# A cross-attention block whose written-out order is exchanged for another one

## The chip, the cores and the metric

The kernel runs on one core of one Trainium2 chip. The metric is the device time of one execution in microseconds (us). A core has five engines with instruction queues of their own: PE multiplies matrices, DVE (VectorE), ACT (ScalarE) and POOL (GpSimd) work element by element, and SP issues the transfers between the chip's memory and the on-chip memory (SBUF). PE's results land in the banks of a second on-chip memory (PSUM).

## The reference

One transformer layer with cross attention, all in float32. The inputs are `x` and `ctx`, each 8 x 256 x 512 (8 batches of 256 tokens, 512 features), and a mask over the context's tokens; there are 16 heads of 32, and the inner width is 2048. What is computed, cut to its core:

```python
x = layer_norm(hidden_states, ln1_w, ln1_b)
q = x @ q_w + q_b;  k = ctx @ k_w + k_b;  v = ctx @ v_w + v_b      # per head
attn = softmax(where(mask, q @ k.T / sqrt(32), lowest))
hidden = (attn @ v) @ cproj_w + cproj_b + hidden_states
y = layer_norm(hidden, ln2_w, ln2_b)
y = gelu(y @ fc_w + fc_b) @ proj_w + proj_b
return hidden + y
```

## The kernel before, in words

The tokens are worked through in two groups, `g` = 0 and 1, of 1024 tokens (four batches) each. In each group the kernel transposes the context (`turned`, L710, for group 0), forms keys, values and queries, runs attention in 16 units of four heads and one batch (`scores`, L1009, and `attend`, L1057), applies the output projection, and then the two large products: `fc` (L1184, 512 to 2048, with gelu) and `proj` (L1248, 2048 to 512). The two groups overlap: attention of group 1 runs beside `fc` of group 0, and so on.

Every large product is made from seven smaller ones instead of eight (Strassen's scheme in Winograd's form). `quad` (L848) writes one such scheme: products `P1` to `P7` go to three PSUM banks X, Y and W, and element-wise steps `t1`, `t2`, `t3`, `c11`, `c12`, `c21`, `c22` take them out and add them up. The sums of operands that the scheme needs are made beforehand by `sums` (L827) through `plus` (L621): for example `kws1` to `kws4` from the key weights, `fw...` from the weights of fc, `pw...` from those of proj, `y...` and `z...` from the activations. For fc and proj the scheme is used on two levels, so that `fc104_P3` is the product P3 within the outer product 4 of the fc of group 1 (half 0), and `pd11_P5` the product P5 within the outer product 1 of the proj of group 1. The sums of the weights are stored to the chip's memory once (`fcd`, `prd`) and loaded again when they are used (`fl...`, `pl...`).

The helpers that the profile names: `mm` (L636) issues the matmuls of a product (L639), `plus` an addition (L630, on POOL L628 in two halves where it is 1024 wide), `take` and `copy` (L606, L619) a copy out of PSUM, `load` (L590, L593) and `store` (L596, L599) one transfer each on SP. `less` inside `scores` (L1042 on DVE, L1047 on POOL) takes the row maxima off the scores ahead of the exponential.

No scheduler orders the work when the kernel is built. The order is written out by hand in a string `PROGRAM`: 2953 words, one for each operation. The method `run` (L94) reads it. Each engine issues its operations in the order in which their words stand, and a letter behind a colon names the engine where two can do it: `V` is DVE, `A` ACT, `G` POOL. A second string, `PLACES` (L355), gives 1286 buffers their place: a number is a slot of SBUF (or a bank of PSUM), and `C0` or `W1` a bank lent from the other set of banks. A wide SBUF slot of 1024 is an even number n and covers the half slots n and n + 1. Two buffers with one place follow each other: the later one is filled when the last reader of the earlier one is done. PSUM has banks W (3) and C (5).

```python
        for word in PROGRAM.split():
            name, _, e = word.partition(":")
            o = ops.pop(name)
            o.eng = letters[e] if e else o.alts[0][0]
...
    with tc.manual_schedule():
        for o in order:
            o.fn(o.eng)
```

All transfers go through the one queue of SP, in order: a load whose slot is not free yet holds up all that stands behind it. Eight transfers can be outstanding.

At the start, `cq...` loads the context, `turn_c0_...` transposes it, `vw..` and `kw..` load weights of values and keys, and `v0_0_P1` is the first large product. At the end, `ending` (L1293) finishes the last quarter: `tr1_..` transposes results on DVE into `tq`, `out1_..` adds the residual, `so1_..` store `tq` in pieces of 128 KB; the last product `pd14_P4` comes out in the layout of the output (in the profile its tile is `pd_V`), `turn_o..` are PE transposes of the rest, `ot..` and `oz` add, and `st1`, `st00` and `st01` store.

Of the kernel before, what the change touches and what calls it, by code (L numbers as in the profile page):

```python
# [124 lines left out]
cq0_00_1 cq0_00_0 vw00 cq0_01_1 cq0_01_0 rows8 rows7 cq0_10_0 turn_c0_00 rows0 turn_c0_10 c0_00:A cq0_10_1 c0_10:V  # L125
cq0_11_0 small v0_0_P1 cq0_11_1 kw01 turn_c0_11 fw0_01_0 v0_1_P1 c0_11:A vw11 rows5 turn_c0_01 rows2 turn_c0_30
vw10 c0_01:A turn_c0_20 mk c0_30:A c0t1:G c0_20:V v0_0_t1:A vw01 turn_c0_21 v0_1_t1:V turn_c0_31 fw0_11_1 k0_0_P2
c0_21:V rows3 c0_31:V c0t2:V kw10 k0_1_P2 rows4 kw11 c0t3:V kw00 rows6 v0_0_P2 vws1:V fw0_10_0 c0t4:V fw0_00_0
v0_1_P2 vws2:V fw0_00_1 kws1:V xt0_3 rows1 k0_1_P1 fw0_10_1 kws2:V mk~1 xt0_0 kws3:V fw0_11_0 v0_0_c11 fw0i1_1:G
v0_1_P6 fw1_00_1 vws4:V xt0_2 fw0i1_2:V fw0s3:V fw1_00_0 k0_0_P1 v0_1_t2:A xt0_6 fw0i7_1:V fw1_10_0 v0_1_c11  # L130
fw0i7_2:G fw1_11_0 cols v0_1_P5 cols~1 qw10 k0_0_t1:V qw11 fw0i7_4:V fw0s1:V xt0_1 v0_0_P6 v0_1_t3:A fw1_11_1
fw0s2:V fw1_10_1 xt0_5 k0_0_P6 fw0i6_3:V xt0_4 k0_1_t1:V fw0i6_1:G cb fw0i5_1:G v0_1_P3 k0_0_t2:V kws4:G fw0i1_4:V
k0_1_P6 stats_x0_30 fw0i1_3:G fw1i1_1:V stats_x0_00 fw0i6_2:G k0_0_P5 fw1i1_3:V k0_1_t2:A xt0_7 v0_0_t2:V fw1i1_2:G
fw0_01_1 stats_x0_10 fw1i1_4:G fcd0_1_True aggr_x0_30 k0_1_P5 fw1i4_1:V qw01 aggr_x0_00 stats_x0_01 fw1i4_2:G
fw1_01_0 fw0i6_4:V fcd0_6_False stats_x0_11 k0_1_P7 k0_1_t3:A fw1_01_1 aggr_x0_01 fw0i7_3:V k0_0_t3:A eps_x0_0
fcd0_7_False stats_x0_31 pow_x0_0 qw00 aggr_x0_31 k0_1_P3 fw1i4_4:G k0_1_c22 fcd0_7_True fw0i5_2:G aggr_x0_11
fcd0_5_False nb_x0_0 k0_0_c11 fw0i5_4:G norm_x0_01:A v0_0_P5 aggr_x0_10 k0_1_c11 fw0i2_1:G norm_x0_00:A fw1i4_3:V
k0_1_c12:A fw0i2_2:V k0_0_P7 eps_x0_1 eps_x0_3 fw0i5_3:V stats_x0_20 pow_x0_3 stats_x0_21 pow_x0_1 k0_0_P3 nb_x0_3
nb_x0_1 fw0i2_3:V norm_x0_31:A aggr_x0_20 aggr_x0_21 eps_x0_2 fw0i2_4:V norm_x0_10:A pow_x0_2 k0_0_c22 fcd0_2_True
k0_1_P4 v0_0_t3:V fw1i2_1:G fcd1_4_True k0_0_c12:A fcd0_6_True norm_x0_11:A nb_x0_2 fw0s4:V kd0_0_11 k0_0_P4  # L140
fcd1_1_True vws3:V norm_x0_20:A fcd0_3_False fw1i2_2:V fcd0_5_True norm_x0_21:A qws1:V turn_x0_10 norm_x0_30:A
fw1i2_4:G k0_0_c21 turn_x0_00 x0_10:A turn_x0_20 turn_x0_30 x0_20:A v0_0_P3 x0_30:V qws3:G xt1_2 cb1_02 x0_00:V
v0_1_c12:A fw0i3_1:V turn_x0_31 fw1i2_3:V turn_x0_11 fw0i3_2:V x0_31:A turn_x0_21 fw1s1:V turn_x0_01 q0_0_P1
x0_01:A qws2:G v0_0_c12:V fcd1_5_False x0_21:A k0_1_c21 fcd1_2_True fw1i5_3:G cb1_20 x0_11:A q0_0_P2 cb1_03
q0_0_t1:A x0t1:V q0_1_P1 fw0i3_3:V q0_0_c11 x0t2:V s000 fw0i3_4:V x0t3:V q0_0_P6 ev000_11 ev000_31 fw1s3:V xt1_3
ev000_10 ev000_01 cb1_12 q0_0_P7 x0t4:V kd0_0_21 q0_0_t2:A fcd1_7_False q0_1_t1:A fw1s2:V ev000_21 ev000_00 q0_0_P5
mx000_0 fw1s4:G fcd1_6_False cb1_10 q0_1_P6 q0_0_t3:A ev000_30 q0_0_c22 ev000_20 stats_x1_10 fcd1_3_False q0_1_P2
fw1i3_3:V fw1i5_1:V q0_1_t2:V fw1i5_2:G mx000_1 q0_0_P4 fw1i6_1:G qws4:G q0_1_c11 q0_1_P5 q0_0_c21 fw1i5_4:V mt000
fw0i4_3:G fcd1_5_True mc000_3 mc000_2 s020 cb1_13 mc000_1 fw1i6_3:G fold000 cb1_00 fw1i7_1:V q0_0_P3 md000 ev020_30
fw0i4_1:V ev020_21 fw1i7_2:V cb1_23 ev020_00 fw0i4_2:G cb1_21 ev020_10 fw1i7_4:G ev020_20 cb1_01 q0_1_P7 ev020_01  # L150
cb1_11 fw1i3_1:G ev020_31 q0_0_c12:A mx020_1 fw1i6_2:G ev020_11 s002 fw1i3_2:G mm000 mx020_0 fw0i4_4:G v0_1_P7
fw1i7_3:G mt020 stats_x1_11 mc020_2 mc020_3 fw1i6_4:G q0_1_t3:V ev002_30 ev002_11 fw1i3_4:G aggr_x1_10 aggr_x1_11
v0_0_P7 mc020_1 q0_1_c22 ev002_01 ev002_00 fold020 ev002_10 eps_x1_1 md020 ev002_31 pow_x1_1 ev002_20 q0_1_P3
fcd1_7_True v0_0_c22 ev002_21 cb1_31 nb_x1_1 mx002_0 less000_1:G mm020 s022 mx002_1 cb1_33 cb1_22 v0_0_P4 ev022_20
cT1_10 cb1_32 ev022_30 cT1_00 ev022_11 cb1_30 less000_0:G ev022_31 mt002 v0_1_c22 ev022_21 q0_1_P4 ev022_00 mx022_1
mc002_2 ev022_01 ev022_10 less020_0:G mx022_0 v0_1_P4 mt022 q0_1_c21 mc022_2 mc022_3 s010 mc022_1 v0_0_c21 mc002_3
exp000_0 less020_1:G cT1_01 k1_0_P1 fold022 mc002_1 ev010_20 q0_1_c12:V md022 exp000_1 v0_1_c21 fcd1_6_True cT1_20
fcd1_3_True k1_1_P1 ev010_10 ev010_31 fold002 ev010_11 cT1_11 md002 cT1_30 av000 vd0_0_11 k1_0_t1:A cT1_21 mm022
c1t1:G ev010_21 kd0_0_12 ev010_01 cT1_31 ev010_30 kd0_1_12 exp020_0 k1_0_P2 r000 mm002 ev010_00 exp020_1 att000
c1t2:V s030 norm_x1_11:A c1t3:V av020 xd1_3 ev030_10 norm_x1_10:A fcd0_4_True less022_1:G mx010_1 ev030_11 xd1_2  # L160
# [195 lines left out]
cq0_00=42 cq0_10=78 cq0_01=10 cq0_11=0 ps_cols=4 ps_c0_00=2 c0_00=36 ps_c0_10=3 ps_c0_20=3 c0_10=48 ps_c0_30=2  # L356
ps_c0_01=0 c0_01=16 ps_c0_11=3 ps_c0_21=4 c0_11=72 ps_c0_31=0 xt0_0=71 xt0_1=46 xt0_2=47 xt0_3=60 xt0_4=15 xt0_5=14
# [1141 lines left out]
```

## Time and profile before

| | before |
|---|---|
| device time, median of 3 runs | 665.8 us (665.53 to 665.96) |
| span of the profiled execution | 662.0 us |
| PE busy | 654.6 us, 99% |
| DVE busy | 585.7 us, 88% |
| POOL busy | 374.8 us, 57% |
| ACT busy | 342.4 us, 52% |
| moved by DMA | 144.84 MB, 219 GB/s on average |

The span reaches from the first to the last record of one execution. The profile shows no separate device time for this one execution; the device times of the three runs are 3.5 to 4.0 us above its span.

Busy times are totals over the whole span. The profile's windows give the same for a stretch of time: its start and end, its length, the busy time of PE, PE's weight loads (PEld), DVE, ACT and POOL with the number of their instructions, the clock granted to PE, the share of the DMA engines' time and the GB/s. A row of a list of waits names an engine, a tile and line that waited, what it waited for, and the time in total, the number and the longest. A row of a timeline gives start, length, engine, line, operation and tiles, with the idle time before it and what ended that.

### The profile page before, as it was taken

Reading aid. Unit: us, or ns where it says so; the run is one execution under the profiler, and the core shown is the slowest. Engines: PE = TensorE matmul, PEld = TensorE weight load, DVE = VectorE, ACT = ScalarE, POOL = GpSimd, SP = SyncE. Lnnn points to the kernel's source line nnn. Section 1 sums busy time; section 2 is a strip of 40 time slices with the busy share of each in tenths; the row PEclk is TensorE's granted clock in tenths of the full one; section 3 lists DMA queues with packets and bytes.
Section 4 is the critical chain, followed back from the end, with each engine's and each line's share of the span. In section 5 each row is a group of like instructions: output and inputs, shape, how many; then the busy total and the mean of one; then the engine's idle time right before and its main releaser. Section 6 shows DMA issues by size and latency. Waiting matters only on the chain.

```text
span 662.0 us, 11469 instructions
## 1 busy us (share of the span) xinstructions
PE 654.6 (99%) x3925; PEld 490.0 (74%) x3925; DVE 585.7 (88%) x980; ACT 342.4 (52%) x702; POOL 374.8 (57%) x340
## 2 busy tenths in 40 slices
PE   8999999999999999999999999999999999999997
PEld 7746554477544776777688888888888888888887
DVE  2998799999999999999999998997789787998775
ACT  2046479799999899866995572030020013930000
POOL 1262773646888997699958774423535217720260
PEclk9999999999999999999999999999999999999999
DMA  8999888786574467886878698889978779359366
GB/s 250 311 356 307 211 197 291 267 255 125 144 241 161 144 202 234 263 268 197 266 249 273 198 235 225 289 269 230 195 193 241 190 201 242 93 142 240 106 141 111
DMA packets 206586, 144.84 MB, mean 219 GB/s; under 512 B 117008, under 2 KB 166976, under 8 KB 206528
## 3 DMA queue, kind: packets, MB, share of 16 engines
q1 hardware_dynamic: 206528, 144.11, 76.8%
q8 instruction: 31, 0.51, 0.3%
q14 instruction: 27, 0.22, 0.1%
HBM read 104.10 MB, written 39.98 MB: 218 GB/s over the span
## 4 chain that ended last, share of the span: by engine, by line
PE 92%; DVE 5%; ACT 1%; DMA 1%; issue 0%; SPq 0%; POOL 0%; DVEq 0%; ACTq 0%
PE pd_X L639 15%; PE fc_X L639 14%; PE fc_W L639 8%; PE av L639 7%; PE pd_W L639 7%; PE s L639 4%; PE o_X L639 4%; PE q_X L639 4%; PE k_X L639 4%; PE v_X L639 4%; PE pd_Y L639 4%; PE fc_Y L639 4%; PE q_W L639 2%; PE k_W L639 2%; PE v_W L639 2%; PE o_W L639 2%
## 5 line engine op out<-in xcount | busy, mean ns | idle before, releaser
L1047 POOL TENSOR_TENSOR pr<-pr,mm 128x512 f32<-128x512 f32 x84 | 110.4, 1346 | 22.8 <-DMA mm<-md 9.2
L619 ACT ACTIVATE pr<-s,cols 128x256 f32<-128x256 f32 x256 | 104.5, 482 | 21.8 <-PE s L639 15.8
L1022 DVE TRANSPOSE_TENSOR_REDUCE mx<-pr 128x32 f32<-128x1024 f32 x64 | 77.6, 1223 | 3.3 <-ACT pr L619 3.3
L1227 ACT ACTIVATE h<-h,cols 128x256 f32<-128x256 f32 x128 | 54.1, 498 | 36.7 <-DVE h L630 36.6
L1050 ACT ACTIVATE pr<-pr 128x1024 f32<-128x1024 f32 x64 | 66.9, 1069 | 3.4 <-POOL pr L1047 2.8
L630 DVE TENSOR_TENSOR h<-fc_X,h 128x512 f32<-128x512 f32 x80 | 52.8, 679 | 6.2 <-PE fc_X L639 5.5
L630 DVE TENSOR_TENSOR h<-fc_W,h 128x512 f32<-128x512 f32 x48 | 32.0, 679 | 5.8 <-PE fc_W L639 5.3
L639 PE MATMUL av<-pr,ones 128*32 128x256 f32 x512 | 34.2, 384 | 0.7 <-ACT pr L1050 0.6
L1029 ACT COPY mx<-mx 32x64 f32<-32x64 f32 x96 | 23.1, 243 | 19.8 <-DVE mx L1026 15.8
L1042 DVE TENSOR_TENSOR pr<-pr,mm 128x1024 f32<-128x1024 f32 x22 | 30.8, 1407 | 0.0
L628 POOL TENSOR_TENSOR z1i<-h,z1i 128x512 f32<-128x512 f32 x4 | 5.7, 1440 | 40.4 <-PE pd_X L639 40.4
L639 PEld LDWEIGHTS av<-pr,ones 128*32 128x32 f32 x512 | 14.1, 109 | 18.5 <-issue 6.7
L630 POOL TENSOR_TENSOR h<-h,fl 128x512 f32<-128x512 f32 x9 | 11.5, 1295 | 24.6 <-DVE fl L630 15.0
L639 PE MATMUL fc_W<-y1i,fl 128*128 128x256 f32 x100 | 24.6, 380 | 0.0
L639 PE MATMUL fc_X<-y1i,fl 128*128 128x256 f32 x88 | 21.6, 381 | 0.0
L639 PEld LDWEIGHTS fc_W<-y1i,fl 128*128 128x128 f32 x100 | 18.9, 190 | 2.9 <-DVE h L630 0.3
L639 PE MATMUL pd_W<-z0i,pl 128*128 128x256 f32 x88 | 20.6, 379 | 0.0
L1030 DVE TENSOR_REDUCE mx<-mx 32x32 f32<-32x256 f32 x32 | 18.4, 574 | 1.4 <-ACT mx L1029 1.3
L639 PE MATMUL pd_X<-z0i,pl 128*128 128x256 f32 x80 | 18.9, 379 | 0.0
L606 ACT COPY fl<-fc_X 128x512 f32<-128x512 f32 x6 | 3.5, 580 | 29.5 <-PE fc_X L639 29.2
L639 PEld LDWEIGHTS fc_X<-y1i,fl 128*128 128x128 f32 x88 | 16.6, 190 | 2.6 <-ACT h L606 0.2
L639 PEld LDWEIGHTS pd_W<-z0i,pl 128*128 128x128 f32 x88 | 16.7, 190 | 2.3
(595 smaller groups left out, 1815.6 us busy)
## 6 DMA issues: line engine op xcount, KB each, us to landing
mm<-md SPq DMA_DIRECT2D x32, 512.0 KB, 5.1
pl<-prd SPq DMA_DIRECT2D x47, 256.0 KB, 4.2
fl<-fcd SPq DMA_DIRECT2D x41, 256.0 KB, 4.0
fl<-prd SPq DMA_DIRECT2D x24, 256.0 KB, 3.8
fw<-in_L_xattn_fc_w_dram SPq DMA_DIRECT2D x16, 256.0 KB, 4.9
pw<-in_L_xattn_proj_w_dram SPq DMA_DIRECT2D x32, 128.0 KB, 3.6
hid<-in_x_dram SPq DMA_DIRECT2D x8, 512.0 KB, 4.8
hd<-hid SPq DMA_DIRECT2D x8, 512.0 KB, 3.4
```

The costliest lines, as they stand in the source:

```text
L606: (nc.scalar.copy if e == "ACT" else nc.vector.tensor_copy)(to(), of_())
L619: lambda e: nc.scalar.activation(to(), of_(), AF.Identity, bias=bias(), scale=1.0))
L628: nc.gpsimd.tensor_tensor(to()[:, ts(k, 512)], in0()[:, ts(k, 512)], in1()[:, ts(k, 512)], op)
L630: E[e].tensor_tensor(to(), in0(), in1(), op)
L639: nc.tensor.matmul(o(), l(), r(), start=first, stop=True, skip_group_check=True)
L1022: T.op(f"mx{u}_{h}", [("DVE", 1.126)], [(pr[h], None)], [(mx, [h])], lambda e, h=h: nc.vector.tensor_reduce(tile_of(mx)[:, 0:64].rearrange ...
L1029: lambda e, a=a: nc.scalar.copy(tile_of(mx)[0:32, 64 + 64 * a : 128 + 64 * a], tile_of(mx)[32 * a : 32 * a + 32, 64:128]))
L1030: T.op(f"fold{u}", [("DVE", 0.38)], [(mx, [2, 3, 4, 5])], [(mx, [6])], lambda e: nc.vector.tensor_reduce(tile_of(mx)[0:32, 320:352], tile_ ...
L1042: nc.vector.tensor_tensor(p_, p_, m_[:, :, None, :].to_broadcast([P, 2, 2, S]), ALU.subtract)
L1047: E[e].tensor_tensor(p_, p_, at(M, j)[:, None, :].to_broadcast([P, 2, S]), ALU.subtract)
L1050: lambda e, h=h: nc.scalar.activation(tile_of(pr[h]), tile_of(pr[h]), AF.Exp), table="exp")
L1227: lambda e, f=f, b=b, c=c: nc.scalar.activation(at(h[f][b], c), at(h[f][b], c), AF.Gelu_apprx_tanh, bias=col(c_fcb + f * 4 + c), scale=1.0 ...
```

## The change

All functions stay as they are. `PROGRAM` and `PLACES` are replaced as wholes. The 2953 words are the same but for the engine letters. Of the operations, 223 change engine: 98 go from DVE to POOL, 67 from POOL to DVE, 34 from ACT to DVE and 24 from DVE to ACT. By number of operations DVE goes from 913 to 892, ACT from 692 to 682 and POOL from 250 to 281; PE keeps its 500 and SP its 598. Nearly every buffer has another slot or bank. PE's operations keep their order roughly: 101 of 500 stand at the same position in PE's own sequence, 357 within three places of it, and none is more than 34 places away.

The first words of the order, before and after:

```diff
-cq0_00_1 cq0_00_0 vw00 cq0_01_1 cq0_01_0 rows8 rows7 cq0_10_0 turn_c0_00 rows0 turn_c0_10 c0_00:A cq0_10_1 c0_10:V
-cq0_11_0 small v0_0_P1 cq0_11_1 kw01 turn_c0_11 fw0_01_0 v0_1_P1 c0_11:A vw11 rows5 turn_c0_01 rows2 turn_c0_30
...
+cq0_00_1 small cq0_00_0 turn_c0_00 turn_c0_10 cq0_01_1 cq0_01_0 vw00 c0_10:V vw10 vws3:V turn_c0_01 c0_00:A cq0_11_0
+turn_c0_11 c0_11:V vw11 cq0_11_1 cq0_10_1 c0_01:V c0t1:V rows5 v0_0_P1 v0_1_P1 kw00 cq0_10_0 turn_c0_21 turn_c0_31
...
```

The last words (in before, seven large products stand behind `pd12_P4`, in the new order two; the words from it on are shown):

```diff
...
-out1_01:V pd12_P4 pl14_5 pd12_c12 tr1_01 out1_00:V pd17_12~1:V pd14_P6 so1_01 tr1_13 so1_03 so1_22 so1_20 pd13_P4
-pd14_t2 so1_23 pd12_c21 z1i4_3:V so1_31 so1_02 pd14_P5 pd13_c21 tr1_12 out1_11:V tr1_11 pd14_P2 tr1_10 out1_10:V pd14_t3
-so1_13 pd14_P7 so1_12 pd14_c11 so1_10 so1_11 so1_00 pd14_P3 pd14_c22 pd14_c21 turn_o00 pd14_c12 turn_o10 turn_o11 ot00
-turn_o01 ot11 pd14_P4 st00 ot10 ot01 st1 oz st01
...
+out1_11:V pd12_P4 so1_31 pd14_t3 tr1_11 pd14_P3 pd14_c21 pd14_c22 rl1 turn_o11 pd12_c21 tr1_10 turn_o10 so1_33
+turn_o00 out1_10:V pd14_c12 turn_o01 ot00 so1_21 out1_00:G so1_02 so1_01 so1_00 ot10 so1_12 so1_03 ot11 so1_13 so1_11
+ot01 st1 st00 so1_10 z1i4_4:G pd14_P4 oz st01
```

Among the products of group 1 this sequence stands on PE in the new order: `pd11_P6`, `fc104_P3`, `fc104_P4`, `fc114_P4`, `fc114_P3`, `pd11_P5`. Some of the places that change, cut to single entries:

```diff
-pl06_3=86
-h0_20=72
-pl11_6=57
-pl11_5=35
-pl12_2=59
-pl15_6=44
+pl06_3=39
+h0_20=38
+pl11_6=32
+pl11_5=32
+pl12_2=38
+pl15_6=38
```

More of the change, by code (lines that the diff above doesn't have):

```diff
@@ L350 @@
-pd14_P6 so1_01 tr1_13 so1_03 so1_22 so1_20 pd13_P4 pd14_t2 so1_23 pd12_c21 z1i4_3:V so1_31 so1_02 pd14_P5 pd13_c21
-tr1_12 out1_11:V tr1_11 pd14_P2 tr1_10 out1_10:V pd14_t3 so1_13 pd14_P7 so1_12 pd14_c11 so1_10 so1_11 so1_00
-pd14_P3 pd14_c22 pd14_c21 turn_o00 pd14_c12 turn_o10 turn_o11 ot00 turn_o01 ot11 pd14_P4 st00 ot10 ot01 st1 oz st01
+cq0_00_1 small cq0_00_0 turn_c0_00 turn_c0_10 cq0_01_1 cq0_01_0 vw00 c0_10:V vw10 vws3:V turn_c0_01 c0_00:A cq0_11_0
+turn_c0_11 c0_11:V vw11 cq0_11_1 cq0_10_1 c0_01:V c0t1:V rows5 v0_0_P1 v0_1_P1 kw00 cq0_10_0 turn_c0_21 turn_c0_31
@@ new lines @@
+pd06_P2 pd02_t2 pd02_P7 aggr_y1_00 pd02_P5 eps_y1_0 pd06_t3 pd06_c22 pd06_c11 aggr_y1_20 pd05_P2 z0i6_4:V z0t4_0:V
+aggr_y1_11 z0i5_1:V pow_y1_0 eps_y1_3 pl02_3 pow_y1_3 pd06_P4 pd02_t3 pd02_c22 pl06_3 z0t4_2:V hd6 nb_y1_0 pd05_t1
+nb_y1_3 eps_y1_2 z0t3_3:V z0t4_1:V pow_y1_2 pd06_P3 pd02_P3 z0t3_0:V pd06_c21 z0i5_3:V pd04_P1 pl07_3 pd05_c11 hd4
+pd02_P4 nb_y1_2 norm_y1_21:A pl05_4 norm_y1_31:A eps_y1_1 pl04_7 z0i5_2:V norm_y1_00:V pl05_6 hd7 pd05_P7 pd06_c12
+pl03_6 pl03_2 pd05_P6 pow_y1_1 pl07_1 pd02_c21 nb_y1_1 norm_y1_10:A z0i5_4:V yd1_7 norm_y1_20:A yd1_5 pd05_t2
@@ new lines @@
+rq1_12 pd11_P2 gelu1_120 pd11_P6 fc113_c21 fc104_P3 fc114_c22 pl13_7 pl17_2 gelu1_122 gelu1_312 gelu1_230 gelu1_121
+z1t1_0:V fc104_c22 gelu1_030 fc117_12~1:G gelu1_333 pl11_5 gelu1_311 fc104_P4 z1i1_3:G gelu1_201 pd11_c11 pd11_t2:V
+pl17_1 z1t3_0:V gelu1_331 fc104_c21 gelu1_320 gelu1_132 fc114_P4 z1i1_4:G gelu1_232 pl11_4 fc114_P3 gelu1_123
+fc114_c21 gelu1_231 gelu1_301 gelu1_300 pd11_P5 gelu1_330 pd17_P1 z1t1_1:V z1t3_1:V z1t3_3:V pd11_t3:V pd11_P7
+fc114_c12 pd13_P1 pd11_c22 pd11_P3 pl15_2 z1i7_1:G z1i7_2:V fc104_c12 gelu1_302 pd17_t1:A pd11_P4 z1i7_3:V z1t2_0:V
```

649 lines of the change are left out of this document (316 added, 333 removed).

## The prediction

> **What bounds the kernel now.** I read the page first (busy shares and the chain that ended last), then PE's share window by window, then the list of what PE waited for.
>
> ```profile
> span 662.0 us, 11469 instructions
> PE 654.6 (99%) x3925; PEld 490.0 (74%) x3925; DVE 585.7 (88%) x980; ACT 342.4 (52%) x702; POOL 374.8 (57%) x340
> PE 92%; DVE 5%; ACT 1%; DMA 1%; issue 0%; SPq 0%; POOL 0%; DVEq 0%; ACTq 0%
> ```
>
> PE is busy for 654.6 of 662.0 us and makes 92% of the chain. The windows (start and end, length, then busy time of PE, PEld, DVE, ACT and POOL, the granted clock, the DMA share and GB/s) show where the other 7.4 us lie.
>
> ```profile
> 0.00:17.00 17.00, 15.28 (x92) 12.34 (x93) 4.70 (x8) 4.02 (x6) 3.31 (x10) 1.00 0.81 251
> 180.00:210.00 30.00, 30.00 (x224) 13.47 (x226) 29.45 (x46) 28.88 (x59) 25.55 (x16) 1.00 0.67 211
> 240.00:270.00 30.00, 28.50 (x306) 20.25 (x299) 29.24 (x68) 28.74 (x52) 25.49 (x26) 1.00 0.73 234
> 248.00:265.00 17.00, 15.95 (x220) 10.68 (x208) 16.42 (x42) 16.50 (x24) 12.49 (x12) 1.00 0.77 237
> 265.00:281.00 16.00, 15.51 (x121) 11.34 (x121) 15.56 (x29) 13.23 (x28) 11.33 (x13) 1.00 0.82 267
> 281.00:298.00 17.00, 16.38 (x120) 12.69 (x120) 16.65 (x28) 11.03 (x27) 16.39 (x19) 1.00 0.81 263
> 646.00:658.00 12.00, 12.00 (x66) 10.66 (x66) 8.23 (x19) 0.00 (x0) 0.00 (x0) 1.00 0.72 114
> 658.00:662.00 4.00, 0.64 (x6) 0.45 (x5) 0.42 (x1) 0.00 (x0) 0.00 (x0) 0.95 0.38 119
> ```
>
> Idle PE: 1.7 us in the head, 1.05 + 0.49 + 0.62 = 2.16 us in 248 to 298, and 3.4 us after the last product. What is left over is 0.1 us in 600. In 180 to 210 PE never pauses although DVE and ACT are nearly full: those two work ahead of PE and are not late. PE's waits:
>
> ```profile
> PE ps_y L726 <- DVE att L630: 1.2, 2, 1.0
> PE first L651 <- DVE warm L646: 1.0, 1, 1.0
> PE av L639 <- ACT pr L1050: 0.6, 1, 0.6
> PE v_X L639 <- DMA vw<-in_L_xattn_v_w_dram: 0.5, 1, 0.5
> PE ps_c L726 <- DMA cq<-in_ctx_dram: 0.2, 1, 0.2
> ```
>
> No transfer makes PE wait after the head. The same products are run in both orders, so whatever is decided is decided by four things: the head, the stretch 248 to 298, loads that come late, and the tail.
>
> **The change part by part.** Every PE product stays what it is, and none moves far: of the 500 named PE operations, 357 stand within three places of where they were. That costs nothing by itself. Of the 223 operations on another engine, 98 go from DVE to POOL, 67 back, 34 from ACT to DVE and 24 back. At each form's mean duration DVE loses 23 us of work and POOL gains 60; I take 0 for this, covered by PE, which POOL at 57% and DVE at 88% both trail. What it costs if that cover is gone is a rival below.
>
> *Head.* Rows of PE and of the queue:
>
> ```profile
> 4.44 1.93 PE L726 MATMUL ps_c<-ident,cq 128*128 128x128 f32 x8 [0.20 <-DMA cq<-in_ctx_dram]
> 7.51 1.97 PE L639 MATMUL v_X<-vw,c 128*128 128x256 f32 x8 [0.53 <-DMA vw<-in_L_xattn_v_w_dram]
> 9.31 0.60 PE L726 MATMUL ps_c<-ident,cq 128*128 128x128 f32 x4
> 9.75 0.60 PE L639 MATMUL v_X<-vw,c 128*128 128x256 f32 x2
> 8.82 0.37 SPq L593 DMA_DIRECT2D kw<-in_L_xattn_k_w_dram  x1
> ```
>
> Before, the queue issues `cq cq vw cq cq`; the product `v0_0_P1` waits for the third load and starts at 7.51, after two transposes of `c`. The queue keeps eight transfers outstanding, and `kw` is the thirteenth, so the fifth load has landed by 8.8; the fourth, between 7.5 and 8.8, I put at 8.15. After, the order is `cq cq cq cq vw`, and two more transposes stand ahead of `v0_0_P1`: one of them needs the fourth load. A transpose of four records takes 9.75 - 9.31 = 0.44 us. So `v0_0_P1` starts at 8.15 + 2 x 0.44 = 9.03 (`vw` has landed by 8.8), 1.52 us later, of which the two transposes, 0.88, are work that before is done afterwards. Net **+0.6**. Bounds: -0.2 if all loads come 0.8 earlier, for the first transfers are no longer shared with the weights; +1.4 if `vw` lands one place, 0.8, later than I have it.
>
> *248 to 298.* Here PE trails DVE, ACT and POOL. Counting for each product the work that its feeders' queues must do between the last input and the product, the order of before is short by over 1 us for 45 operations and the order of after for 24, and the worst goes from 3.4 to 2.4. I take about half of the 2.16 us of idle time off: **-1.0**. Bounds: -2.2 (all of it) and +1.1 (the sum of POOL's work and of DVE's on two SBUF tensors goes from 33.9 to 35.0 us in 240 to 270).
>
> *Loads with little time.* A weight load is issued when the last product that reads its slot is done; the time until its own product is the products in between, at this pace:
>
> ```profile
> 363.53 3.45 PE fc_X L639 x16
> 640.20 1.89 PE L639 MATMUL pd_X<-z1t,pl 128*128 128x256 f32 x8
> 641.93 1.89 PE L639 MATMUL pd_X<-h,fl 128*128 128x256 f32 x8
> ```
>
> An fc product is 4 records, 3.45 / 4 = 0.86 us, and a pd product 8, 641.93 - 640.20 = 1.73 us. In before the shortest such time that I count past the head is 4.97 us. In after four are much shorter. `pl11_5` has slot 32, from `pl11_6`: between `pd11_P6` and `pd11_P5` stand four fc products, 3.45 less 0.2 for the release, 3.24. `pl15_6` has the slot of `pl12_2`, with `pd16_P3` and `pd16_P4` between: 3.24. `pl11_6` is queued on SP behind a load that waits for `fc113_P4`: 3.66. `pl06_3` has the slot of a hidden half that `z0t4_0` frees: 3.70. Three more are at 4.32 to 4.52. Against these stand the landing times (KB, then median us from issue):
>
> ```profile
> pl<-prd SPq DMA_DIRECT2D x47, 256.0 KB, 4.2
> fl<-fcd SPq DMA_DIRECT2D x41, 256.0 KB, 4.0
> fl<-prd SPq DMA_DIRECT2D x24, 256.0 KB, 3.8
> pl<-fcd SPq DMA_DIRECT2D x6, 256.0 KB, 4.6
> vws<-fcd SPq DMA_DIRECT2D x4, 256.0 KB, 2.9
> ```
>
> At 4.0 us PE would wait 0.76 + 0.76 + 0.34 + 0.30 = 2.16 us; at 2.9 nothing; at 4.6, 1.36 + 1.36 + 0.94 + 0.90 and 0.5 for the other three, 5.1. I take the middle row, **+2.2**, since three of the four loads are rows of this kind. PE is full there, so what it waits nothing gives back. [...]
>
> *Tail.* Rows of PE, DVE and the queue:
>
> ```profile
> 652.29 1.89 PE L639 MATMUL pd_W<-z1i,fl 128*128 128x256 f32 x8
> 654.01 1.89 PE L639 MATMUL pd_X<-z1t,pl 128*128 128x256 f32 x8
> 655.74 1.11 PE L1312 MATMUL ps_o<-ident,po 128*128 128x128 f32 x8
> 656.69 1.95 PE L639 MATMUL pd_V<-fl,z1i 128*128 128x128 f32 x16
> 649.57 0.45 DVE L1339 STREAM_TRANSPOSE tq<-po 128x256 f32<-128x256 f32 x1
> 650.05 0.69 DVE L630 TENSOR_TENSOR tq<-tq,rq 128x512 f32<-128x512 f32 x1
> 645.57 10.16 SPq L599 DMA_DIRECT2D out_dram<-tq  x12
> 656.72 2.78 SPq L599 DMA_DIRECT2D out_dram<-ot  x3
> ```
>
> Before, twelve 128 KB stores of `tq` go out from 645.6 to 655.7, and only three of `ot` follow the last product. After, the last products are `pd12_P4`, `pd14_P3`, the four turns of `po`, `pd14_P4` (the `pd_V` row). Counted back from 656.69 at these durations, `pd12_P4` begins at 656.69 - 0.95 - 1.73 - 1.73 = 652.28 and ends at 654.0; its addition (0.4, as the transpose), transpose 0.45 and addition 0.69, with 0.1 between each, end at about 655.9. `so1_12` waits for them, and behind it on SP stand `so1_03`, `so1_13`, `so1_11`, `so1_10` and the `ot` stores: five stores of 131 KB, 655 KB. The window 646 to 658, made of such stores, moves 114 GB/s at a share of 0.72, 158 at a share of one: 4.15 us, or 5.75 at 114. To it come 0.5 to issue the first; the 0.52 MB of `ot`, 1.95 us at the 267 GB/s of the window 265 to 281, of which I let 0.45 overlap; and 1.2 of completion (the last `ot` store of before is issued by 656.72 + 2.78 = 659.5, the span ends 2.5 later, and of these I count 0.5 for its start and 0.8 for its 131 KB at 158 GB/s). The span then ends at 655.9 + 0.5 + 4.15 + 1.5 + 1.2 = 663.25 to 664.85, that is +1.25 to +2.85 on 662.0: **+2.0**. Bounds: 0, if the stores overlap wholly with the product's own tail, and +3.5, if `ot` queues behind all five at the slower rate.
>
> *Sum.* 0.6 - 1.0 + 2.2 + 2.0 = +3.8 us: a span of 665.8. The profile gives no time beside the span for its own execution; the median of the runs, 665.8, is 3.8 above it, and I carry these 3.8 over: **669.6 us**.
>
> **The rivals.** *Faster:* the transfers, on which three of my four terms rest, run at the quiet rates. The head's loads come 0.8 earlier (-0.2), the weights land in 2.9 us (0), the stores drain as fast as they are issued (0). With the stretch at -1.0 that is -1.2 and 664.6, and up to its -2.2, 663.4. It decides where the median landing falls below 3.2 us, the smallest of the four rooms. For it: the `vws` row reaches 2.9. Against it: three rows with 112 loads stand at 3.8 to 4.2, and the windows' DMA shares are 0.7 to 0.8, so the queue isn't quiet.
>
> *No change:* the stretch gains all of its 2.2, the tight loads cost a third (0.7) and the tail its lower figure: 0.6 - 2.2 + 0.7 + 1.25 = +0.35, 666.2. That lies within 1.3 us of 665.8, the 0.2% that a measurement of this kernel can tell. It needs three terms on the same side at once.
>
> *Much slower:* POOL and DVE hold each other up, and PE is fed by a pair that can't work at once. Rows, minimum, median and maximum in ns:
>
> ```profile
> L1042 DVE TENSOR_TENSOR pr<-pr,mm x22: 1169/1217/2324, 105.3 to 377.2; 128x1024 f32<-128x1024 f32 x22
> L1047 POOL TENSOR_TENSOR pr<-pr,mm x84: 1258/1278/2767, 85.1 to 318.2; 128x512 f32<-128x512 f32 x84
> ```
>
> The same operation takes up to 1.1 us more on DVE and 1.5 more on POOL, about one operation of the other. At the undisturbed durations, POOL's work and DVE's on two SBUF tensors in the stretch that is 150 to 180 us in before adds up to 29.1 us for 28.8 us of products, and 36.2 in after. If they never overlap and nothing moves ahead, that is +7.4; with my sum less the stretch's gain it gives 665.8 + 4.8 + 7.4 = 678. In 240 to 270 before has 33.9 of it for 28.7 us of products and PE loses 1.5 there, so of 5.2 too many 1.5 showed; at that share 7.4 costs 2.1, and 672.7. [...]
>
> **How the numbers follow.** My forecast, 667.1 to 672, has 0.45; the much slower case 0.22; no change 0.13; faster 0.20, its low end being 661 if the head and the tail gain as well. Slower is 0.67 then. The range, 662.5 to 676.5, leaves out the lower end of faster (0.08) and the upper end of the port (0.08).
>
> **What would show it.** Head: the `v_X` row near 9.0 instead of 7.51. Loads: waits of `pd_X` for DMA on `pl` in PE's list, 0.3 to 1 us each. Stretch: under 2.2 us of idle PE between 248 and 298. Tail: `tq` stores still being issued after 656 of the old scale, and over 3.4 us from PE's end to the span's. It is wrong if new idle windows of PE appear whose releaser is POOL or DVE, or if the loads land in under 3.2.

## The result: 5.9% slower

The new order takes 702.8 us (701.6 to 709.9, four runs); the kernel before takes 665.7 beside it. The ratio is 1.0589, its 95% interval 1.0532 to 1.0647. I had forecast 669.6 us and a range up to 676.5: the direction was right, the size wrong by a factor of nearly ten.

The page of the changed kernel, its first part and the chain that ended last (all lines of the code stand 7 lower: L632 was L639, L623 was L630, L621 was L628):

```profile
span 700.4 us, 11497 instructions
PE 663.5 (95%) x3925; PEld 491.6 (70%) x3925; DVE 603.7 (86%) x959; ACT 333.9 (48%) x688; POOL 460.0 (66%) x388
PE 37%; DVE 21%; DMA 19%; SPq 9%; issue 5%; ACT 3%; POOL 3%; DVEq 0%; ACTq 0%; POOLq 0%
```

The span grew by 38.4 us. PE's idle time went from 7.4 to 700.4 - 663.5 = 36.9 us, 29.5 more, and its busy time for the same 3925 instructions by 8.9. PE's share of the chain fell from 92% to 37%. Two engines became busier by more than the change in their work: DVE, of whose work I had counted 23 us away, is busy 18 us longer, and POOL 85 us longer where I had counted 60.

PE's waits in the changed kernel (what it waited for, us in all, times, the longest):

```profile
PE pd_X L632 <- DVE po L623: 2.6, 1, 2.6
PE fc_W L632 <- DVE h L623: 2.6, 1, 2.6
PE pd_W L632 <- DMA pl<-prd: 2.2, 1, 2.2
PE fc_X L632 <- DMA fl<-fcd: 1.8, 3, 0.7
```

There is no one big wait; these are the first four of 29 rows. PE stops all along the span, for element-wise work and for transfers. One of the stops of 2.6 us, step by step, on PE, DVE and POOL:

```profile
447.42 1.78 PE L632 MATMUL pd_X<-z0i,pl 128*128 128x256 f32 x7 [2.65 <-DVE po L623]
```

```profile
437.46 1.22 DVE L623 TENSOR_TENSOR z0i<-z0t,z0t 128x1024 f32<-128x1024 f32 x1
438.59 1.22 DVE L623 TENSOR_TENSOR z0i<-h,h 128x1024 f32<-128x1024 f32 x1
439.73 2.30 DVE L623 TENSOR_TENSOR z0i<-z0t,z0i 128x1024 f32<-128x1024 f32 x1
441.95 2.29 DVE L623 TENSOR_TENSOR z0i<-h,z0i 128x1024 f32<-128x1024 f32 x1
444.16 2.28 DVE L623 TENSOR_TENSOR z0i<-z0t,z0t 128x1024 f32<-128x1024 f32 x1
...
446.96 0.40 DVE L623 TENSOR_TENSOR po<-pd_X,po 128x256 f32<-128x256 f32 x1
```

```profile
439.68 3.48 POOL L621 TENSOR_TENSOR z0t<-h,h 128x512 f32<-128x512 f32 x2 [3.22 <-PE pd_W L632]
443.12 4.44 POOL L621 TENSOR_TENSOR z0t<-h,z0t 128x512 f32<-128x512 f32 x2
```

A sum of 1024 takes DVE 1.22 us until POOL starts one at 439.68, and 2.3 beside POOL's from then on; POOL's own pair of pieces, 2.55 us undisturbed, takes 3.5 to 4.4. The product that PE wants next needs the small `po` operation, which stands in DVE's queue behind the three slow sums, so PE stands still for 2.65 us.

The same kinds of operation over the whole span, from the views of the tiles `z0i` and `z1t`, first before, then after (number, minimum, median and maximum in ns, first and last start), and below them a group of the changed kernel (busy time, mean ns):

```profile
L630 DVE TENSOR_TENSOR z0i<-h,h x5: 1216/1219/1220, 404.5 to 457.8; 128x1024 f32<-128x1024 f32 x5
L630 DVE TENSOR_TENSOR z1t<-h,z1t x6: 1212/1215/1219, 585.6 to 620.0; 128x1024 f32<-128x1024 f32 x6
```

```profile
L623 DVE TENSOR_TENSOR z0i<-h,h x6: 1210/1226/2279, 423.4 to 490.8; 128x1024 f32<-128x1024 f32 x6
L623 DVE TENSOR_TENSOR z1t<-h,z1t x6: 1216/1703/2296, 620.6 to 668.6; 128x1024 f32<-128x1024 f32 x6
```

```profile
L623 DVE TENSOR_TENSOR h<-fc_X,h 128x512 f32<-128x512 f32 x80 | 52.6, 679 | 5.9 <-PE fc_X L632 5.2 <-PE fc_W L632 0.2
```

In the order of before these two kinds are never slowed. Other rows of the same two views reach 1.53 and 1.66 us there, so some sums meet POOL in it too, but none of these takes 2.3. The last row, an operation of which one operand comes from PSUM, has a mean of 679 ns in both kernels, and none of its 80 takes more than 693 in either: it is not slowed.

The head and the tail of the changed kernel, on PE and the queue:

```profile
8.37 1.09 PE L719 MATMUL ps_c<-ident,cq 128*128 128x128 f32 x8 [1.67 <-DMA cq<-in_ctx_dram]
9.30 3.62 PE L632 MATMUL v_X<-vw,c 128*128 128x256 f32 x16
691.42 1.95 PE L632 MATMUL pd_V<-pl,z1i 128*128 128x128 f32 x16
```

```profile
685.58 7.65 SPq L592 DMA_DIRECT2D out_dram<-tq  x9
696.06 0.56 SPq L592 DMA_DIRECT2D out_dram<-fl  x1
```

PE ends at 691.42 + 1.95 = 693.4, and the span 7.0 us later, where before it was 3.4.

### The profile page after: what moved, and what is told of

It reads as the page before. It is cut to its first block, busy times and chain, and to the rows that moved or that the text cites. A ratio compares the mean times of both kernels' runs of the same rounds, so it can differ in the third digit from the quotient of the medians.

```text
span 700.4 us, 11497 instructions
## 1 busy us (share of the span) xinstructions
PE 663.5 (95%) x3925; PEld 491.6 (70%) x3925; DVE 603.7 (86%) x959; ACT 333.9 (48%) x688; POOL 460.0 (66%) x388
## 4 chain that ended last, share of the span: by engine, by line
PE 37%; DVE 21%; DMA 19%; SPq 9%; issue 5%; ACT 3%; POOL 3%; DVEq 0%; ACTq 0%; POOLq 0%
PE pd_X L632 10%; SPq L586 8%; PE pd_W L632 5%; DVE mx L1015 4%; PE fc_X L632 3%; DVE h L623 3%; PE fc_W L632 3%; DMA mm<-md 3%; PE q_X L632 2%; PE pd_Y L632 2%; DMA fw<-in_L_xattn_fc_w_dram 2%; PE av L632 2%; DMA fl<-fcd 2%; PE o_X L632 2%; ACT pr L612 2%
## 5 line engine op out<-in xcount | busy, mean ns | idle before, releaser
L1040 POOL TENSOR_TENSOR pr<-pr,mm 128x512 f32<-128x512 f32 x92 | 123.7, 1374 | 43.5 <-DMA mm<-md 33.2
L1220 ACT ACTIVATE h<-h,cols 128x256 f32<-128x256 f32 x128 | 56.0, 501 | 49.9 <-DVE h L623 38.2
L623 DVE TENSOR_TENSOR h<-fc_X,h 128x512 f32<-128x512 f32 x80 | 52.6, 679 | 5.9 <-PE fc_X L632 5.2
L632 PE MATMUL av<-pr,ones 128*32 128x256 f32 x512 | 35.0, 384 | 1.6 <-ACT pr L1043 0.9
L623 DVE TENSOR_TENSOR h<-fc_W,h 128x512 f32<-128x512 f32 x48 | 31.7, 678 | 2.9 <-PE fc_W L632 2.6
L632 PEld LDWEIGHTS av<-pr,ones 128*32 128x32 f32 x512 | 14.6, 109 | 18.3 <-issue 7.5
L1035 DVE TENSOR_TENSOR pr<-pr,mm 128x1024 f32<-128x1024 f32 x18 | 24.1, 1351 | 3.2 <-DMA mm<-md 3.1
L632 PE MATMUL pd_W<-z0i,pl 128*128 128x256 f32 x88 | 21.1, 389 | 3.3 <-DMA pl<-prd 2.2
L623 POOL TENSOR_TENSOR tq<-tq,rq 128x512 f32<-128x512 f32 x9 | 12.0, 1333 | 17.4 <-DVE h L599 9.4
L811 ACT ACTIVATE xn_y<-hid,rs_y 128x512 f32<-128x512 f32 x11 | 8.5, 813 | 30.6 <-DVE rs_y L797 30.6
L632 PE MATMUL pd_X<-z0i,pl 128*128 128x256 f32 x80 | 20.1, 397 | 2.6 <-DVE po L623 2.6
L623 POOL TENSOR_TENSOR h<-h,fl 128x512 f32<-128x512 f32 x9 | 14.3, 1606 | 10.9 <-DVE fl L623 9.9
L632 PEld LDWEIGHTS pd_W<-z0i,pl 128*128 128x128 f32 x88 | 16.8, 193 | 6.3 <-POOL z0i L621 2.5
L621 POOL TENSOR_TENSOR z0i<-h,z0i 128x512 f32<-128x512 f32 x8 | 12.8, 1622 | 12.1 <-DVE z0i L623 12.0
L632 PEld LDWEIGHTS pd_X<-z0i,pl 128*128 128x128 f32 x80 | 15.9, 201 | 5.7 <-DVE po L623 3.0
L623 DVE TENSOR_TENSOR h<-fc_Y,h 128x512 f32<-128x512 f32 x24 | 16.2, 679 | 3.7 <-PE fc_Y L632 3.5
L800 POOL TENSOR_TENSOR rs_y<-rs_y,neg_half 128x2 f32<-128x2 f32 x8 | 8.2, 1039 | 16.6 <-DVE rs_y L797 16.0
```

The costliest lines, as they stand in the source:

```text
L621: nc.gpsimd.tensor_tensor(to()[:, ts(k, 512)], in0()[:, ts(k, 512)], in1()[:, ts(k, 512)], op)
L623: E[e].tensor_tensor(to(), in0(), in1(), op)
L632: nc.tensor.matmul(o(), l(), r(), start=first, stop=True, skip_group_check=True)
L1035: nc.vector.tensor_tensor(p_, p_, m_[:, :, None, :].to_broadcast([P, 2, 2, S]), ALU.subtract)
L1040: E[e].tensor_tensor(p_, p_, at(M, j)[:, None, :].to_broadcast([P, 2, S]), ALU.subtract)
L1220: lambda e, f=f, b=b, c=c: nc.scalar.activation(at(h[f][b], c), at(h[f][b], c), AF.Gelu_apprx_tanh, bias=col(c_fcb + f * 4 + c), scale=1.0 ...
```

## Experiments

**Which part of the change costs.** The change has three parts that can be put together anew: the order of the words, their engine letters, the places. First the new order and places with the old letters, then the old order and places with the new letters:

```diff
 PROGRAM (the new order)
-... out1_10:V ... out1_00:G ... z1i4_4:G ...
+(the same words in the same order, each with the letter that it has in before)
```

> The new order and the new places, with the 223 operations on the engine that they had before. Theory 1 (DVE and POOL shut each other out, because the new order sets work of two SBUF tensors on both at the same time): the overlap is a matter of the order, not of the 223 alone, so the time falls by a part only, to 680 to 697 us, and POOL's and DVE's mean durations fall with it. Theory 2 (the order and the places leave too little time between an operation and its user, whatever the engine): 697 to 706 us. If the letters alone are the cause: 664 to 672 us.

Measured: 760.7 us, ratio 1.140 (1.133 to 1.147). All expectations missed: it is 58 us slower than the new kernel.

> The order and the places of before, with the engines of the new kernel for the 223 operations. Theory 1: the 60 us of work that POOL gets now lies beside DVE's in an order that wasn't made for it; DVE's 1024-wide operations go from 1.22 to about 2.3 us where they meet, and the time is 675 to 695 us. Theory 2: the order of before has its reserves, so 664 to 670 us.

Measured: 707.5 us, ratio 1.061 (1.057 to 1.065), against the expectation of the second theory and above that of the first. The new letters alone cost the old order as much as the whole change costs. So letters and order belong together, in both kernels, and either is spoilt by the other's letters. That contradicts "the letters alone" as well as "the order alone". (No run has the new order with the old places: the order was never changed by itself.)

Each buffer in the slot free the longest, in the new kernel:

```diff
-PLACES = (the new places)
+PLACES = (for every SBUF buffer, in order of first use, the free slot whose last use stands furthest back in PROGRAM)
```

> The new kernel with its order and engines, and each buffer of SBUF in the slot that has been free the longest. Theory 1: loads come earlier, but DVE and POOL are as slow as in the new kernel: 693 to 703 us. Theory 2, as far as it rests on the slots: the weight loads are no longer late, which took 14 us of PE's time: 685 to 691 us.

Measured: 763.0 us, ratio 1.145 (1.138 to 1.151), a miss of both. The queue of SP shows it:

```profile
SPq L586 <- PE pd_X L632: 74.5, 31, 7.1
```

In the changed kernel the same row has 15.1 us in 4 waits. A slot whose last use stands far back in the list of words can still be read late in time, and then the load holds up the queue. The run says that places can cost 60 us; it doesn't tell whether the new places cost anything, and that stays open.

**Is it that POOL shuts DVE out?** POOL's sums read two columns only and fill the rest with a constant:

```diff
 def fn(e):      # plus, and likewise less
-    nc.gpsimd.tensor_tensor(to()[:, ts(k, 512)], in0()[:, ts(k, 512)], in1()[:, ts(k, 512)], op)
+    nc.gpsimd.tensor_tensor(to()[:, k : k + 2], in0()[:, k : k + 2], in1()[:, k : k + 2], op)
+    for _ in range(m):                       # m = 1, then 2
+        nc.gpsimd.memset(to()[:, k + 2 : k + 512], 0.25)
```

> The new kernel, but POOL's sums and differences are left out: in place of each, POOL works on two columns only and fills the rest with a constant, so that it hardly reads SBUF (its output is not the reference's). Theory 1: DVE's 1024-wide operations stay at 1.22 us all through, DVE's busy time falls by about 40 us, and with it most of the 37 us: 665 to 680 us. Theory 2: DVE's durations or not, loads and queue order keep the time at 690 to 703 us.

> As the run with constants on POOL (its sums and differences are left out, two columns are worked on, the rest is filled), but filled twice, so that a piece of 512 takes POOL about 0.35 + 2 x 0.52 = 1.4 us, no less than the 1.28 of the undisturbed sum. Theory 1 (it was that POOL's reading no longer shuts DVE out): 680 to 690 us, as with one filling (684.4). If the 18 us came from POOL being faster: 695 to 703 us.

Measured: 684.4 us with one filling (ratio 1.026, 1.022 to 1.029), between the two expectations, and 683.2 with two (1.028, 1.023 to 1.033), in the range of the first theory. POOL's busy time was 254 us in the one and 419 in the other, and the time the same, so how long POOL works doesn't matter here. Rows of the run with two fillings, the span and DVE's sums:

```profile
span 677.8 us, 12193 instructions
PE 657.0 (97%) x3925; PEld 493.5 (73%) x3925; DVE 551.2 (81%) x959; ACT 333.2 (49%) x688; POOL 418.8 (62%) x1106
```

```profile
L626 DVE TENSOR_TENSOR z0i<-h,h x6: 1214/1219/1226, 406.1 to 470.0; 128x1024 f32<-128x1024 f32 x6
L626 DVE TENSOR_TENSOR z1t<-h,z1t x6: 1212/1215/1219, 598.9 to 646.1; 128x1024 f32<-128x1024 f32 x6
```

No sum in these rows takes more than 1.23 us any more. Over the whole kernel a single one of 1024 is still slow, 3.38 us at 390.4, beside one of the few sums of POOL that the fillings leave in place (L1411). DVE's busy time falls by 603.7 - 551.2 = 52.5 us, and 702.8 - 683.2 = 19.6 us of the time are gone, about half of the loss (20.5 by the two ratios). POOL still writes SBUF through most of its 419 us here, so its writing doesn't shut DVE out; its sums, which read, do. The edit takes away the reading and the adding together, so that it is the reading is not shown by these runs. The sums are slow beside POOL's sums and not beside its fillings, and the 2.3 us are 1.22 and most of a POOL piece of 1.28.

The same on the old order with the new letters, on the old kernel, and on the new order with the old letters:

> The order and the places of before with the new engines (707.5 us), and POOL's sums and differences left out for two fillings each, of no less time. Theory 1: the letters cost 40 us because POOL's added work shuts DVE out, so they cost little once it doesn't read: 664 to 676 us. If DVE or POOL are simply in another order than PE needs: 690 to 708 us.

Measured: 682.0 us (1.026, 1.022 to 1.031) for 707.5: 25.5 us of that loss (23 by the ratios), between the two expectations.

> The kernel before with POOL's sums and differences left out for two fillings each, of no less time. Theory 1: PE is busy 99%, and DVE's 49 us of stretch are hidden, so there is little to win: 661 to 667 us. If POOL's longer pieces (1.4 us for 1.28) matter by themselves: over 668 us.

Measured: 662.7 us beside 664.2, ratio 0.9966 (0.9937 to 0.9995). As expected. In the kernel before the shutting out is there too: without it DVE's busy time falls from 585.7 to 570.3 us, by 15.4 (the 49 of the expectation were too many), against 52.5 in the new kernel. It costs next to nothing there: PE, busy 99%, is idle 7.1 us for 7.4, and there is little left to win.

> The new order and places with the engines of before (760.7 us), and POOL's sums and differences left out for two fillings each. If the shutting out makes most of that loss too: under 715 us. If an operation that stands in the order for one engine comes too late in the queue of the other, whatever POOL reads: 730 to 755 us.

Measured: 741.6 us (1.113, 1.108 to 1.119) for 760.7, as expected in the second case: 19 us here as well, and 76 are left. Which letters cost, in the old order: the 98 to POOL, the 67 to DVE, the 58 between ACT and DVE.

```diff
 PROGRAM (the old order)
-98 words :V      -67 words :G      -58 words :A or :V
+98 words :G      +67 words :V      +58 words :V or :A      (one group in each run)
```

> The kernel before with only the 98 operations moved from DVE to POOL. POOL gets some 100 us more, all of it reading SBUF, DVE loses about half of that. Theory 1: the shutting out costs more than DVE is relieved: 690 to 710 us, DVE's stretch over 80 us. If DVE's load decides: 660 to 668 us.

Measured: 695.9 us (1.046, 1.042 to 1.050), in the range of the first theory. PE's longest wait in it, 7.07 us, and what DVE and POOL do ahead of it:

```profile
193.34 10.29 DVE L1033 TENSOR_TENSOR pr<-pr,mm 128x1024 f32<-128x1024 f32 x1
193.00 2.50 POOL L619 TENSOR_TENSOR x1t<-x,x1t 128x512 f32<-128x512 f32 x2
195.46 2.50 POOL L1038 TENSOR_TENSOR pr<-pr,mm 128x512 f32<-128x512 f32 x2
197.91 4.63 POOL L1404 TENSOR_TENSOR hid<-hid,cb 128x1024 f32<-128x1024 f32 x2
205.64 1.93 PE L630 MATMUL av<-pr,ones 128*32 128x256 f32 x16 [7.07 <-DVE att L621]
```

One sum of DVE, 1.22 us when nothing holds it up, takes 10.29 us here. POOL does six pieces without a gap and without being slowed, up to 202.54, and DVE ends at 203.63, about the length of its own sum later. `att`, for which PE waits, stands behind that sum in DVE's queue. In the stop at 447.4 both engines were slowed, DVE's sums to 2.3 us and POOL's pairs to 3.5 and 4.4; here only DVE was. What decides that stays open.

> The kernel before with only the 67 operations moved from POOL to DVE. Theory 1: there is less to collide, so DVE's stretch falls under 45 us and the time stays at 664 to 674 us. If what counts is that PE's next operand stands behind more work in the queue of DVE: 680 to 700 us.

Measured: 685.2 us (1.031, 1.026 to 1.036), in the range of the other theory.

> The kernel before with only the 58 operations that change between ACT and DVE. Neither engine reads SBUF in POOL's place, so nothing is shut out by these. If only the shutting out costs: 664 to 668 us. If an operation costs because it comes at another time in the queue of its new engine: 670 to 685 us, with PE waiting for ACT and DVE.

Measured: 673.2 us (1.010, 1.003 to 1.017), in the range of the second case. The busy times from its page, and PE's longest wait:

```profile
PE 657.3 (98%) x3925; PEld 491.5 (73%) x3925; DVE 591.3 (88%) x990; ACT 337.0 (50%) x692; POOL 375.1 (56%) x340
```

```profile
PE av L630 <- DVE att L621: 1.4, 1, 1.4
```

Every group costs, whichever way it moves work: 30, 20 and 10 us against before. How much of it is shutting out can be counted from the traces, as the time that DVE's sums of two SBUF tensors take above 1.22 us for 1024 columns, 0.68 for 512 and 0.41 for 256. That is 17.4 us in before, 53.1 in the changed kernel and 4.3 in it with two fillings; in these three runs it is 52.7, 22.4 and 16.7. So in the third nothing new is shut out, and POOL is as busy as before (375.1 us, before 374.8). What is left as its cause is that an operation comes at another moment in the queue of its new engine, or takes another time there (the run doesn't tell these apart), and PE waits for what stands behind it. That is the second mechanism.

**Are the loads late?** 47 weight loads further ahead in the queue, without and with the fillings:

```diff
 PROGRAM (the new order), 47 words like these
-yb1_02 yb1_30 pl07_7
+pl07_7 yb1_02 yb1_30
```

> The new kernel with 47 weight loads further ahead in the queue of SP, by 0.5 to 3 us, as far as their slots are free by then; all else as in the new kernel. If late loads cost by themselves what PE's waits for them add up to (15.5 us): 688 to 695 us. If the loads are late because all before them is, or DVE's lateness takes over where a load comes sooner: 697 to 703 us.

Measured: 709.8 us (1.067, 1.060 to 1.074): no gain at all.

```profile
PE fc_W L632 <- DVE h L623: 4.8, 3, 3.8
...
PE pd_W L632 <- DMA pl<-prd: 1.9, 1, 1.9
```

PE's waits for weight loads add up to 5.3 us in its list instead of 8.6, and DVE's lateness takes their place (`h` had 2.6 us in one wait).

> The new kernel with both edits: POOL's sums and differences left out for two fillings each, and the 47 weight loads earlier. With the fillings alone 683.2 us, and there PE still waits 6.7 us for weight loads. If what is left of the loss is loads behind others in the queue: 674 to 679 us. If another wait takes their place, as it did without the fillings: 681 to 686 us.

Measured: 687.8 us (1.033, 1.029 to 1.038), against 683.2 without the moved loads. A miss of both, though the two intervals overlap. PE's waits for weight loads fall from 5.6 to 3.2 us in its lists, and others come up: `fc_Y` waits 3.3 us for DVE, `k_X` 1.7 for ACT. In the run with two fillings alone the stop that is left at 475 us reads so on the queue and PE:

```profile
463.06 6.36 SPq L586 DMA_DIRECT2D yb<-yd  x6
469.55 0.78 SPq L586 DMA_DIRECT2D pl<-prd  x1
```

```profile
474.85 1.62 PE L635 MATMUL pd_W<-z0i,pl 128*128 128x256 f32 x3 [3.02 <-DMA pl<-prd]
```

The load is issued at 469.6 behind six `yb` loads, which take 6.4 us to be issued though none waits for data, and lands at 474.7. What holds these issues up is not shown; the DMA engines have a share of 1.01 over the 40 us from 440 to 480. So the next repair puts 27 transfers that are used late further back, and takes up the tail:

```diff
 PROGRAM (the new order)
-fl101_2 hd5 rq0_20 ... yb1_21 ... pl07_7
+hd5 ... yb1_21 ... pl07_7 ... fl101_2 ... rq0_20        (27 words of this kind)
-pd12_c22 so1_23 tr1_12 pd14_P7 so1_30 pd14_P5 ... pd12_P4
+pd12_c22 pd12_P4 so1_23 tr1_12 pd14_P7 so1_30 pd14_P5
```

> The new kernel with POOL's sums and differences left out for two fillings each (683.2 us), and two repairs of its order: 27 transfers that are used 15 us or more after their issue in the stretch of 455 to 512 us stand later in the queue, 11 us ahead of their use, and the tail has pd12_P4 three products earlier and so1_03 ahead of so1_12. If what is left there is the order of a queue that is full: PE's idle 4.9 us of 440 to 520 fall under 1.5, the time from PE's end to the span's end falls from 6.9 to 4 or 5, and the time to 674 to 679 us. If the loads of that stretch land late whatever stands ahead of them: idle stays over 4 there.

> The new kernel, all of its work in place (702.8 us), with the same two repairs. If the shutting out and the queue add up: 693 to 699 us. If DVE's lateness takes over where a load comes sooner, as in the run with the 47 loads: 699 to 705 us.

Measured: 682.3 us (1.026, 1.017 to 1.035) with the fillings, a miss, and 699.2 (1.047, 1.037 to 1.058) with all work in place, at the lower edge of the second expectation. Neither can be told from its base, 683.2 and 702.8. The windows, first of the run with the fillings alone, then with the repairs (the last row of each is the end of the span):

```profile
440.00:480.00 40.00, 36.98 (x165) 32.06 (x164) 25.16 (x44) 5.62 (x8) 17.84 (x36) 0.96 1.01 254
480.00:520.00 40.00, 38.13 (x175) 32.82 (x174) 29.37 (x60) 7.06 (x11) 18.15 (x60) 1.00 1.11 237
667.00:677.80 10.80, 3.90 (x30) 3.37 (x28) 3.26 (x8) 0.00 (x0) 0.00 (x0) 0.92 0.69 129
```

```profile
440.00:480.00 40.00, 39.32 (x181) 34.04 (x180) 28.90 (x48) 5.62 (x8) 18.20 (x38) 1.00 0.92 246
480.00:520.00 40.00, 40.00 (x185) 34.77 (x184) 30.01 (x62) 7.06 (x11) 20.51 (x67) 1.00 0.98 226
520.00:560.00 40.00, 37.88 (x174) 32.65 (x174) 29.73 (x51) 8.18 (x18) 15.61 (x50) 1.00 0.99 229
664.60:675.00 10.40, 6.18 (x39) 5.06 (x37) 4.21 (x11) 0.00 (x0) 0.00 (x0) 1.00 0.74 139
```

At the place of the repair it did what was expected: PE's idle 3.0 + 1.9 us fell to 0.7, and that at the end from 10.8 - 3.9 = 6.9 to 4.2. But 2.1 us came up in the next stretch, where there had been none, in two waits for weight loads: the transfers that were put off have to go somewhere, and the DMA share is still 0.99. So what stands ahead in the queue is shown as the cause of those stops, and shown not to be worth its 5 us by itself.

**Does a stop cost more than its length?** DVE was held up at five places of the old kernel:

```diff
 def fn(e):      # plus, for pd02_c11, pd05_c11, pd07_c11, pd11_c11, pd15_c11
+    for _ in range(HOLD.get(name, 0)):       # 24, 36, 48, 64, 80
+        nc.vector.tensor_copy(warm, ones2)
     E[e].tensor_tensor(to(), in0(), in1(), op)
```

> The kernel before with DVE held up at five places of its quiet second half by 24 to 80 copies of 64 elements (some 2 to 7 us), so that PE stands still for stretches of growing length. Theory: after a stop of over about 2.3 us PE works at half its pace for some us, records 0.43 us apart instead of 0.22, so a stop costs more than its length: PE's busy time grows by 1 to 2 us for each long stop and the clock's mean falls to 0.98 to 0.99. If the pace doesn't depend on the stops: PE's busy time stays at 654 to 656 us.

Measured: 734.0 us (1.102); PE's busy time is 666.8 us, 12.2 more than before for the same instructions, 2.4 for each stop where 1 to 2 were expected, and the mean clock 0.958. The stops became longer than intended, 6.4 to 16.8 us, so this run doesn't show where the slow pace begins. After two of them, of 9.2 and 14.9 us (the column after POOL is the granted clock):

```profile
502.00:507.00 5.00, 4.87 (x12) 3.89 (x13) 4.70 (x13) 0.81 (x1) 0.32 (x1) 0.50 0.00 0
507.00:512.00 5.00, 5.00 (x24) 4.40 (x23) 4.41 (x7) 0.00 (x0) 1.25 (x3) 0.96 0.50 141
631.50:636.50 5.00, 4.85 (x12) 3.88 (x12) 5.00 (x7) 0.00 (x0) 0.00 (x0) 0.50 0.01 3
```

For some 5 us PE gets half its clock and does 12 matmuls where it does 24 otherwise. In the changed kernel much shorter stops were enough, 2.63 us ahead of 292.9 and 2.17 ahead of 493.0 (first the stretch ahead of each fall of the clock, then the stretch at half of it):

```profile
289.42:292.83 3.41, 0.84 (x4) 0.39 (x3) 3.41 (x5) 3.41 (x9) 3.41 (x3) 1.00 1.08 387
292.83:296.25 3.42, 3.35 (x8) 2.41 (x8) 2.83 (x7) 1.02 (x2) 3.42 (x4) 0.50 1.00 320
490.81:494.22 3.41, 1.24 (x7) 1.10 (x7) 3.15 (x3) 0.47 (x1) 2.86 (x2) 1.00 1.09 217
494.22:497.63 3.41, 3.41 (x10) 2.66 (x9) 0.00 (x0) 0.00 (x0) 0.00 (x0) 0.50 1.26 177
```

The stop of 2.65 us at 447.4, above, was followed by the full pace, so the length alone doesn't decide, and the 2.3 us of the expectation, an estimate of mine that no run shows, are no limit. The half clock lasts 3.41 us both times, and the two falls lie 494.22 - 292.83 = 201.39 us apart, 59 times 3.413. PE was busy for 0.84 and 1.24 us of the stretches of 3.41 us ahead of the two falls. The stop at 447.4 lies across two stretches of that length, counted on from the first fall, 443.02 to 446.44 and 446.44 to 449.85, with PE busy for 1.75 and 2.43 us and the clock at 1.00. Counted so over the whole trace of the changed kernel, the clock fell three times, the third at 695.60 behind PE's last matmul, after stretches with PE busy for 0.25, 0.36 and 0.34 of them, and stayed full after 197 others, none of them under 0.51 (busy as the profile has it). In the trace of before, counted from its one fall at 661.59, it fell after a stretch with 0.14 and stayed full after 191, none under 0.71. These are counts in two traces; what sets the clock is not shown by them. The two stretches at half the clock cost 3.4 us together, a part of the 8.9 by which PE's busy time grew.

## Why the prediction was wrong, point by point

*The engines, taken at 0.* This is the step that failed. I wrote that the moved work was covered by PE because DVE at 88% and POOL at 57% both trail. Busy shares and undisturbed durations say nothing of whether the two work at the same time on SBUF. They now did: 19.6 us, by the fillings. I had this as a rival with a chance of 0.22, but priced it for one stretch, 150 to 180, from sums per stretch, and cut even that to 2.1 us at its lower end by the little that it cost before. It happens at many places of the span, and not by the sum of the work: DVE's sums of two SBUF tensors of 1024 took up to 2.3 us for 1.22 beside POOL's, while `h<-fc_X`, with one operand in PSUM, stayed under 0.70. That a port stands behind it, as I named this rival where I gave the range, no run shows.

*"None moves far: that costs nothing by itself."* Wrong too. With nothing new shut out, 58 letters between ACT and DVE cost 9.6 us, and the new letters on the old order still 17.8 (682.0 against 664.2) with the fillings. PE's order hardly moved, but the place of an operation in the queues of DVE, ACT and SP relative to PE's did. The prediction had no term for that.

*Head, +0.6.* `v0_0_P1` starts at 9.30; I had 9.03. PE's idle time in the first 40 us went from 1.7 to 2.8, so +1.1, within the bounds.

*248 to 298, -1.0.* The wrong sign: PE is idle there for 3.7 us instead of 2.16. One of the two longest stops of all stands there, 2.63 us ahead of 292.9, with 3.41 us at half the clock behind it; ahead of it two of DVE's sums of 256 take 1.49 and 1.48 us beside POOL's pieces, for 0.41 undisturbed. The counts of operations short of time were made with undisturbed durations.

*Loads, +2.2.* The mechanism is there, the list wasn't. PE's waits for weight loads add up to 8.6 us in its list of waits (the 14 and 15.5 us in the expectations of two runs are in no list). Of the four that I named only `pl11_6` holds PE up, by 0.8 us where I had 0.34: it landed 4.3 us after its issue. `pl11_5`, `pl15_6` and `pl06_3` landed after 2.7, 2.8 and 3.1, within the times that I had counted, so my 4.0 for these was too long; that is the landing time of the *faster* rival. The long waits stand where the queue is slow, as at `pl07_7` (2.2) behind its `yb` loads, or where all that is ahead is late. And they can't be added to the rest: taken away, something else was late.

*Tail, +2.0.* From PE's end to the span's 7.0 us for 3.4, so +3.6, just past the upper bound of 3.5. Right in kind, nine stores of `tq` being issued from 685.6 to 693.2 and four more stores behind.

*The 3.8 us from span to time.* Too much: in all 17 runs with a time for the profiled execution itself, the time is 1.7 to 2.0 us above the span. It is small beside the miss.

*What is settled and what isn't.* Of the 37 us about 20 are POOL and DVE shutting each other out. In the run with the fillings PE is idle 677.8 - 657.0 = 20.8 us and the old kernel with the same fillings 7.1. Of these 13.7 us more, the windows put 3.6 into the tail, 4.9 into 440 to 520 with its slow queue, 0.6 into the head, and the rest into attention and what follows; PE's busy time is 4.1 longer besides. That the rest comes from the places of operations in the queues of DVE and ACT is argued from the runs with the letters, not shown by undoing it in the new order, and what the new places of the buffers cost stays open. No run that does all of the work beats the kernel before.

## What to carry to other kernels

A written-out order is one plan together with its engine letters and its places: changing the letters alone cost 10 to 58 us here, whichever way the work was moved, and other places alone 60. When work moves between DVE and POOL, look for each pair of sums of two SBUF tensors that will stand beside each other: here DVE's of 1024 took 2.3 us for 1.22 beside POOL's, and one 10.29 beside six pieces of POOL without a gap. To count the pair one after the other, and such a run of pieces as a whole, is an estimate from these two; the sum of busy times can't show it. In the changed kernel one repaired wait handed the stop to the next, with DVE only 86% busy.

## What was not expected of the hardware

POOL shuts DVE out by its sums and not by writing SBUF: with POOL filling instead of adding, and busy for 419 us instead of 460, DVE's sum of 1024 stays at 1.22 us, but for one of 3.38, instead of up to 2.3. Nor need both be slowed: one such sum took 10.29 us beside six pieces of POOL that followed each other without a gap. And a stop of PE can cost more than its length: 2.4 us more of busy time for each of five long stops on average, with the granted clock at 0.50 behind them, and 3.41 us at 0.50 already after stops of 2.63 and 2.17 us, though not after one of 2.65. In the trace of the changed kernel, counted in stretches of 3.41 us, PE is busy for 0.25 to 0.36 of the three ahead of a fall of the clock and for at least 0.51 of the 197 others behind which it stays full; what sets the clock is not shown.
